# Token slots by float16 products, and graph rows broadcast to 128 partitions

## The chip, the core and the metric

The kernel runs on one core of one Trainium2 chip. The core has five engines with instruction streams of their own, which meet only through semaphores: TensorE (PE in the profile; its weight loads are listed apart, as PEld), VectorE (DVE), ScalarE (ACT), GpSimd (POOL) and SyncE (SP), which here issues DMAs only. SyncE, ScalarE and GpSimd can issue DMAs; 16 DMA engines carry them out. On-chip memory has 128 partitions, and a tile has a row in each partition that it uses. [...]

The metric is the device time of one execution, in microseconds. A profile is a further execution, taken with the hardware profiler; its stretch from the first to the last instruction is called the span.

## The reference, cut to what matters

1250 tokens of 768 features pass through a two-layer graph attention network with 20000 edges, a linear attention, and a mixture of eight experts with two experts for each token. The two parts that the change touches are the graph attention and the choice of experts:

```python
def gat_conv(x, src, dst, W, a_src, a_dst, bias, H, C, n):
    h = (x @ W).reshape(n, H, C)
    s_src = (h * a_src).sum(-1)
    s_dst = (h * a_dst).sum(-1)
    e = jax.nn.leaky_relu(s_src[src] + s_dst[dst], NEG_SLOPE)
    emax = jax.ops.segment_max(e, dst, num_segments=n)
    ee = jnp.exp(e - emax[dst])
    denom = jax.ops.segment_sum(ee, dst, num_segments=n)
    alpha = ee / denom[dst]
    out = jax.ops.segment_sum(alpha[:, :, None] * h[src], dst, num_segments=n)
...
probs = jax.nn.softmax(x @ router_w, axis=-1)
gates, idx = jax.lax.top_k(probs, TOPK_ROUTED)
gates = gates / jnp.sum(gates, axis=-1, keepdims=True)
...
g = jax.nn.silu(jnp.einsum('bsd,edh->bseh', x, w_gate))
u = jnp.einsum('bsd,edh->bseh', x, w_up)
expert_out = jnp.einsum('bseh,ehd->bsed', g * u, w_down)
routed = jnp.einsum('bse,bsed->bsd', dense_g, expert_out)
shared = jax.nn.silu(x @ ws_gate) * (x @ ws_up) @ ws_down
alpha = jax.nn.sigmoid(x @ sg_w + sg_b)
return alpha * shared + (1.0 - alpha) * routed
```

The first graph layer has 4 heads of 192 features, the second 2 heads of 96.

## The kernel before

**Tiling.** The tokens lie in 10 tiles of 125 (`NT`, `TP`), on 125 partitions. The transposed, normalised input `xnT` has 6 chunks of 128 features.

**Order of the work.** The code is written in a tile framework. It tracks what reads and writes each tile, sets the semaphores, and a planner with a cost model of its own sorts the instructions onto each engine when the program is built; an instruction may pass others that stand ahead of it in the source if its inputs come earlier in that plan. On the chip the order on each engine is fixed. So independent products stand interleaved on TensorE, and where the plan is off, an engine waits. A tile with `bufs=2` has two buffers; a third use waits until the first is free.

**Stages.** (1) Normalisation, first graph projection `G` and the counting of edges into the dense tables `cntT` and `absent` (0 to about 212 us in the profile). (2) Keys and values of the linear attention (L542), beside the maximum of the first graph layer's scores on VectorE (L489), to 394 us. (3) Queries and the projection (L572, L585), to 582 us. (4) First graph attention (L602 to L632), to 733 us. (5) Second graph layer, beside the products of the graph's output layer `update` (L724), to 897 us. (6) Router and shared expert (L845 to L951), to 990 us. (7) Blocks of routed tokens (L1003), to 1535 us. (8) Combination and output.

**Graph rows.** Each layer needs a row of scores in every partition. `rows` (L460) transposes columns of scores into rows and stores them to DRAM (`g_srow_d`, `g_rrow_d`). `Largest.head` (L480) reads one such row of 1250 back into 125 partitions as `ssb`; ten instructions of VectorE (L489, in `tile`) add the mask `absent` to it and take each destination's maximum. `columns` turns these into a second set of rows. `attend` (L591) reads two half rows of 625, for each half of the destinations and each head, into the tile `r`, on 125 partitions. `r` and `ssb` share a tag, and so two buffers. For each tile of sources ScalarE takes two exponentials of `r` (`ea` L602, `eb` L604), VectorE their maximum (L605) and the product with the counts (`u`, L607), and TensorE multiplies by `u` (`pa`, L624, in the first layer; `pn`, L740, in the second). Both broadcasts are issued by GpSimd. In the second layer, `some` and `fill` offer the planner products of `update` between these steps.

**Slots.** Each token goes to two experts. The blocks have 128 places each, and there are `NBLK` = 26 blocks at most. VectorE works out from the router's scores the place of each token's two entries, `slot` (L897): block times 128 plus the place in it. The blocks need the inverse: which token stands at each place. For that, a table `who` in DRAM is filled early with a mark for nobody (L329); then 20 indirect DMAs of GpSimd, one for each token tile and choice, write each token's number (and, in a second word, the number of its output row) to its slot (L902), and a DMA of SyncE that waits for all 20 reads the table back as `ids` (L908). `gather` (L975) uses `ids` for an indirect DMA that fetches a block's token rows from DRAM into `xin`, and `down` uses its second word to write the results. While this goes on TensorE computes the shared expert (L946), nine pairs of `pg` and `pu`, each 128 rows of hidden features by 375 or 500 tokens. The pairs have two buffers in PSUM, which ScalarE (L949) and VectorE (L950, L951) empty. The first block begins with the transposes of `xin` (L1009) behind the last shared product.

```python
put = nc.gpsimd.indirect_dma_start(
    out=who, out_offset=bass.IndirectOffsetOnAxis(ap=slot[:, r, t:t + 1], axis=0),
    in_=number[:, r, t, :], in_offset=None, bounds_check=NSLOT - 1, oob_is_err=False)
```

Of the kernel before, what the change touches and what calls it, by code (L numbers as in the profile page):

```python
# [8 lines left out]
F32 = mybir.dt.float32  # L9
F16 = mybir.dt.float16  # L10
# [3 lines left out]
I32 = mybir.dt.int32  # L14
AF = mybir.ActivationFunctionType
ALU = mybir.AluOpType
# [28 lines left out]

NBLK = -(-((NE - 2) * NPART - 2 * (-N // PART)) // NPART)
NSURE = -(-(2 * N + NE * PART // 2) // P)
NSLOT = NBLK * P


CO = H2 * (C2 + 1) + 2 * H2
# [11 lines left out]
def gps_block(ctx: ExitStack, tc: tile.TileContext, x, src, dst, norm_g, norm_b, W1, a_src1, a_dst1, b1,  # L63
# [7 lines left out]


    xd = dram.tile([N, D], F32, name="xd")
    who = dram.tile([NSLOT, 2], I32, name="who")

    ys = dram.tile([2 * N + P - TP, D], F32, name="ys")
    xd_t = xd.rearrange("(t p) d -> t p d", p=TP)
    who_b = who.rearrange("(b p) o -> b (p o)", p=P)
    who_p = who.rearrange("(b p) o -> p b o", p=P)


    acc = big.tile([TP, NT, D], F32, name="acc")
# [240 lines left out]
    with tc.tile_pool(name="cnt", bufs=1, reuse_waits="tile") as cp, \  # L323
            tc.tile_pool(name="tokps", bufs=2, space=PSUM, reuse_waits="tile") as ps, \
            tc.tile_pool(name="cntps", bufs=3, space=PSUM, reuse_waits="tile") as pcp:

        nobody = cp.tile([NBLK, P, 2], I32, name="nobody")
        nc.gpsimd.iota(nobody, pattern=[[0, P], [2 * N, 2]], base=0, channel_multiplier=0)
        nc.sync.dma_start(who_b, nobody.rearrange("b p o -> b (p o)"))  # L329

        rest = cp.tile([P - TP, D], F32, name="rest")
        nc.gpsimd.memset(rest, 0.0)
        nc.sync.dma_start(ys[2 * N:, :], rest)
# [138 lines left out]
    class Largest:  # L472
# [5 lines left out]
            self.mx = p3.tile([TP, NT, H], F32, name=f"{name}_mx")  # L478

        def head(self, h):  # L480
            self.ssb = pmx.tile([TP, N], F32, name="ssb")
            nc.gpsimd.dma_start(self.ssb, bass.AP(tensor=self.srow.tensor, offset=self.srow.offset + h * N,
                                                ap=[[0, TP], [1, N]]))

        def tile(self, h, dt):


            junk = pmx.tile([TP, N], BF16, name="junk", bufs=1)
            nc.vector.tensor_tensor_reduce(out=junk, in0=self.ssb, in1=absent[:, dt, :], scale=1.0,  # L489
                                           scalar=-3.0e38, op0=ALU.add, op1=ALU.max,  # L490
                                           accum_out=self.mx[:, dt, h:h + 1])

# [98 lines left out]
    def attend(pw, ss, ss02, rrow, H, begin, step, finish, fill=lambda half: None):  # L591
        for half in range(2):
            for h in range(H):
                r = pmx.tile([TP, 2, W], F32, name="r", tag="ssb")
                nc.gpsimd.dma_start(r, bass.AP(tensor=rrow.tensor, offset=rrow.offset + h * N + half * W,
                                             ap=[[0, TP], [H * N, 2], [1, W]]))
                sums = begin()
                for st in range(NT):


                    ea = pw.tile([TP, W], F32, name="ea", bufs=2)
                    nc.scalar.activation(ea, r[:, 0, :], AF.Exp, bias=ss[:, st, h:h + 1])  # L602
                    eb = pw.tile([TP, W], F32, name="eb", bufs=2)
                    nc.scalar.activation(eb, r[:, 1, :], AF.Exp, bias=ss02[:, st, h:h + 1])  # L604
                    nc.vector.tensor_max(ea, ea, eb)  # L605
                    u = pw.tile([TP, W], F32, name="u", bufs=3)
                    nc.vector.scalar_tensor_tensor(u, ea, 1.0, cntT[:, st, half * W:(half + 1) * W],  # L607
                                                   op0=ALU.min, op1=ALU.mult)
                    step(sums, st, h, u)
                    fill(half)  # L610
                finish(sums, half, h)
# [203 lines left out]
    with tc.tile_pool(name="fln", bufs=2, reuse_waits="tile") as pw, tc.tile_pool(name="flnps", bufs=2, space=PSUM, reuse_waits="tile") as ps:  # L815
# [11 lines left out]
        odd = pw.tile([TP, -(-NBLK // 2), 2], F32, name="odd", bufs=1)  # L827
        nc.gpsimd.iota(odd, pattern=[[0, -(-NBLK // 2)], [1, 2]], base=0, channel_multiplier=0,
                       allow_small_or_imprecise_dtypes=True)
        rev = pw.tile([TP, NT, NE], F32, name="rev", bufs=1)  # L830
        nc.gpsimd.iota(rev, pattern=[[0, NT], [-1, NE]], base=NE, channel_multiplier=0,
                       allow_small_or_imprecise_dtypes=True)
        number = pw.tile([TP, 2, NT, 2], I32, name="number", bufs=1)
        for r in range(2):
            nc.gpsimd.iota(number[:, r], pattern=[[TP, NT], [r * N, 2]], base=0, channel_multiplier=1)
        for ts in (range(NH2, NH2 + 3), range(NH2 + 3, NT)):
            for _ in normed(ts, pw, ps):
                pass
# [57 lines left out]
            nc.vector.tensor_reduce(at[:, r, :], pick, axis=AX.X, op=ALU.add)  # L896
        nc.vector.tensor_copy(slot, at)  # L897

        puts = []
        for t in range(NT):  # L900
            for r in range(2):
                put = nc.gpsimd.indirect_dma_start(  # L902
                    out=who, out_offset=bass.IndirectOffsetOnAxis(ap=slot[:, r, t:t + 1], axis=0),
                    in_=number[:, r, t, :], in_offset=None, bounds_check=NSLOT - 1, oob_is_err=False)
                for p in puts:
                    tc.declare_no_dep(put.ins, p.ins, reason="slots differ")
                puts.append(put)
        get = nc.sync.dma_start(ids, who_p)  # L908
        for p in puts:
            tc.add_manual_dep(get.ins, p.ins.name, mybir.DependencyInfo(  # L910
                mybir.DependencyClass.Sync, mybir.DependencyReason.DATA), reason="all slots")

# [240 lines left out]
```

## Time and profile before

| what | us |
|---|---|
| median of 3 runs (lowest, highest) | 1602.89 (1601.76, 1603.23) |
| the profiled execution | 1604.71 |
| its span | 1603.0 |
| VectorE busy | 721.8 |
| ScalarE busy | 367.9 |
| GpSimd busy | 136.6 |
| 20 indirect DMAs of the slots (L902), first start to last start | 945.3 to 973.9 |
| one of them on GpSimd, median | 1.19 |
| one `r` on GpSimd (issue), median | 1.15 |
| one `ssb` on GpSimd (issue), median | 0.52 |

The mean granted clock of TensorE was 0.986 of full speed. The page gives busy times, the time cut into 40 slices, the DMA queues, the chain of work that ended last, the costliest groups of instructions, and the DMA issues with their median time to landing. In a group's line `out<-in` are the names of the tiles, then come the shape and the count, the busy time, the mean of one in ns, and after the second bar the idle time of the engine just before them with what ended most of it. In the table by stretch each engine has its busy time and, in brackets, its instructions; the last three columns are the granted clock, the share of the 16 DMA engines in use, and GB/s. In the chain of waits a line has the start, the length and what the time went to.

### The profile page before, as it was taken

To read this page: it belongs to the slowest core of one execution; us is meant where nothing else is said; L and a number is where in the kernel's file an instruction comes from. 1 tells how busy PE (TensorE), PEld (TensorE's weight loads), DVE (VectorE), ACT (ScalarE), POOL (GpSimd) and SP (SyncE) were. 2 spreads that over 40 slices of the span, in tenths; PEclk is the share of its full clock that TensorE was granted. 3 is DMA by queue.
4 is the path that set the end of the run, shared out by engine and by line. 5 is a ranking of instruction groups with operands and counts; after the bars stand their busy time and mean duration, and the time that the engine had idled before them with its cause. 6 is when DMAs were issued, how large, how long until landed. Compare 5 with 4: busy or idle time off the path is not lost.

```text
span 1603.0 us, 18665 instructions
## 1 busy us (share of the span) xinstructions
PE 1524.3 (95%) x7123; PEld 854.2 (53%) x7123; DVE 721.8 (45%) x1339; ACT 367.9 (23%) x630; POOL 136.6 (9%) x177
## 2 busy tenths in 40 slices
PE   6899889998999989999899999999999999999987
PEld 5566544444454668996455554444444444444443
DVE  7889639511535359986599631111111111111116
ACT  3222211111101048871186310101011110111100
POOL 2211000000000000000000133000100001000000
PEclk9999989999999999999999999999999999999998
DMA  7100041000301111102111338588888888888727
GB/s 201 40 1 1 2 130 41 30 0 21 89 12 49 40 34 36 39 17 77 32 53 57 98 89 244 211 313 307 305 311 326 307 308 309 312 320 312 269 100 269
DMA packets 98586, 229.03 MB, mean 143 GB/s; under 512 B 12746, under 2 KB 35402, under 8 KB 98493
## 3 DMA queue, kind: packets, MB, share of 16 engines
q1 hardware_dynamic: 84547, 191.68, 34.8%
q0 software_dynamic: 11744, 35.43, 6.8%
q10 hardware_dynamic: 2202, 0.64, 0.3%
q8 instruction: 63, 1.03, 0.3%
q14 instruction: 30, 0.25, 0.1%
HBM read 212.18 MB, written 16.48 MB: 143 GB/s over the span
## 4 chain that ended last, share of the span: by engine, by line
issue 32%; PE 30%; DVE 11%; DMA 8%; POOL 4%; ACT 3%; POOLq 0%; SPq 0%; DVEq 0%; ACTq 0%
PE pp L542 6%; PE pu L585 5%; PE pq L572 5%; DVE junk L489 4%; DMA ys<-y,ids 4%; PE pa L624 4%; DVE ea L605 2%; PE pn L740 2%; PE pn L577 2%; ACT eb L604 2%; ACT ea L602 1%; POOL xin L976 1%; DVE u L607 1%; PE pds L1043 1%; POOL ys L1034 1%
## 5 line engine op out<-in xcount | busy, mean ns | idle before, releaser
L1003 PE MATMUL pgb<-wg,xT 128*64 128x384 f32 (+1 forms) x1056 | 178.8, 488 | 0.5 <-ACT xT L1010 0.5
L1003 PE MATMUL pdb<-wd,hT 128*64 128x384 f32 (+1 forms) x1056 | 175.1, 488 | 1.5 <-SPq L1083 1.5
L1003 PE MATMUL pub<-wu,xT 128*64 128x384 f32 (+1 forms) x1056 | 174.0, 486 | 0.0
L542 PE MATMUL pp<-wkv,xnT 128*125 128x512 f32 x360 | 161.9, 599 | 0.1
L624 PE MATMUL pa<-G,u 125*125 125x199 f32 x800 | 140.4, 336 | 11.1 <-DVE h L632 6.0
L624 PEld LDWEIGHTS pa<-G,u 125*125 125x125 f32 x800 | 135.6, 189 | 16.2 <-issue 7.2
L1003 PEld LDWEIGHTS pub<-wu,xT 128*64 128x64 f32 x1056 | 75.7, 137 | 94.6 <-issue 94.6
L1003 PEld LDWEIGHTS pdb<-wd,hT 128*64 128x64 f32 x1056 | 74.6, 137 | 91.7 <-issue 86.9
L1003 PEld LDWEIGHTS pgb<-wg,xT 128*64 128x64 f32 x1056 | 73.7, 137 | 90.7 <-issue 89.8
L542 PEld LDWEIGHTS pp<-wkv,xnT 128*125 128x125 f32 x360 | 66.0, 190 | 73.9 <-issue 73.5
L421 PE MATMUL ph<-wg,xnT 128*125 128x400 f32 x240 | 101.4, 529 | 2.4 <-PEq L435 2.4
L1022 DVE TENSOR_TENSOR h<-h,pgb 128x384 f32<-128x384 f32 x44 | 24.4, 555 | 171.6 <-ACT h L1021 171.6
L1033 DVE COPY y<-pdb 128x768 f32<-128x768 f32 x22 | 21.1, 958 | 178.9 <-PE pdb L1003 178.9
L604 ACT ACTIVATE eb<-r,g_ss 125x625 f32<-125x625 f32 x120 | 95.0, 817 | 23.0 <-DVE ea L605 23.0
L605 DVE TENSOR_TENSOR ea<-ea,eb 125x625 f32<-125x625 f32 x120 | 94.0, 804 | 13.0 <-ACT eb L604 7.6
L607 DVE SCALAR_TENSOR_TENSOR u<-ea,cntT 125x625 f32<-125x625 f32 x120 | 94.1, 805 | 12.5 <-PE pa L624 8.0
L489 DVE CUSTOM_DVE_ANT_0 junk<-ssb,absent 125x1250 bf16<-125x1250 f32 x60 | 87.8, 1463 | 13.7 <-DMA ssb<-g_srow_d 12.4
L1021 ACT ACTIVATE h<-pgb 128x384 f32<-128x384 f32 x44 | 21.6, 490 | 307.6 <-PE pgb L1003 307.6
L572 PE MATMUL pq<-xnT,wq 128*128 128x500 f32 (+1 forms) x216 | 81.4, 521 | 4.2 <-DMA wq<-in_L_mix_w_qkv_dram 4.2
L1027 DVE TENSOR_TENSOR h<-h,pub 128x384 f32<-128x384 f32 x44 | 24.4, 554 | 134.4 <-PE pub L1003 134.4
L724 PE MATMUL pu<-wu,xnT 128*125 128x384 f32 x240 | 82.7, 490 | 1.8 <-DVE acc L729 1.8
L585 PE MATMUL pu<-wp,at 128*125 128x384 f32 x240 | 80.4, 488 | 1.0 <-DVE acc L588 1.0
(254 smaller groups left out, 1696.1 us busy)
## 6 DMA issues: line engine op xcount, KB each, us to landing
wg<-in_L_ffn_w_gate_dram SPq DMA_DIRECT2D x22, 2304.0 KB, 9.6
wu<-in_L_ffn_w_up_dram SPq DMA_DIRECT2D x22, 2304.0 KB, 11.0
wd<-in_L_ffn_w_down_dram SPq DMA_DIRECT2D x22, 2304.0 KB, 10.0
yg<-ys SPq DMA_DIRECT2D x10, 768.0 KB, 8.6
r<-g_rrow_d POOLq DMA_DIRECT2D x12, 610.4 KB, 8.5
wq<-in_L_mix_w_qkv_dram SPq DMA_DIRECT2D x18, 384.0 KB, 3.6
wkv<-in_L_mix_w_qkv_dram SPq DMA_DIRECT2D x6, 768.0 KB, 4.4
acc<-in_x_dram POOLq DMA_DIRECT2D x10, 375.0 KB, 9.7
```

The lines of the kernel that those rows point to most:

```text
L421: nc.tensor.matmul(ph[:, :2 * CG], xnT[:, k, tok], wg[:, k, s * 2 * CG:(s + 1) * 2 * CG], start=(k == 0), stop=(k == KD - 1))
L489: nc.vector.tensor_tensor_reduce(out=junk, in0=self.ssb, in1=absent[:, dt, :], scale=1.0, scalar=-3.0e38, op0=ALU.add, op1=ALU.max, accum_ ...
L542: nc.tensor.matmul(pp, xnT[:, k, tok], wkv[:, k, :, :], start=(k == 0), stop=(k == KD - 1))
L572: nc.tensor.matmul(pq[:, :qw], wq[:, k, :], xnT[:, k, tok], start=(k == 0), stop=(k == KD - 1))
L577: nc.tensor.matmul(pn[j][:, :qw], kvb[:, pr, j, :], qs[:, :qw], start=True, stop=True)
L585: nc.tensor.matmul(pu[:, s, :HALF], at[:, k, i * TP:(i + 1) * TP], wp[:, k, s * HALF:(s + 1) * HALF], start=(k == 0), stop=(k == KD - 1))
L604: nc.scalar.activation(eb, r[:, 1, :], AF.Exp, bias=ss02[:, st, h:h + 1])
L605: nc.vector.tensor_max(ea, ea, eb)
L607: nc.vector.scalar_tensor_tensor(u, ea, 1.0, cntT[:, st, half * W:(half + 1) * W], op0=ALU.min, op1=ALU.mult)
L624: nc.tensor.matmul(pa[i][:, :CO + 1], u[:, i * TP:(i + 1) * TP], G[:, st, h, :CO + 1], start=(st == 0), stop=(st == NT - 1))
L724: nc.tensor.matmul(pu[:, :HALF], xnT[:, k, t * TP:(t + 1) * TP], wus[s][:, k, :], start=(k == 0), stop=(k == KD - 1))
L1003: nc.tensor.matmul(pt[part, :HALF], rows[:, k, part], w[:, k, s * HALF:(s + 1) * HALF], start=(k == 0), stop=(k == KD - 1))
```

## The change

Two things are changed.

The table `who`, its filling, the 20 indirect DMAs and the reading back are gone. `slot` is cut into its low seven bits (the place in the block) and the rest (the block). For each of the two choices VectorE compares the places of all tokens with 0 to 127 (`spot`, 125 x 10 x 128 in float16) and the blocks with 0 to 25 (`numb`, 125 x 10 x 26), and multiplies the latter by the token's number plus one. Ten products of TensorE, one for each token tile, add up `spot` transposed times `numb` in `pids`: at each place of each block stands the number plus one of the token there, or zero. A few small instructions of VectorE make `ids` of it.

The tiles `ssb` and `r` have 128 partitions instead of 125, and so have the DMAs that fill them; the instructions that read them use the first 125. `r` is issued by SyncE instead of GpSimd.

```diff
-        nobody = cp.tile([NBLK, P, 2], I32, name="nobody")
-        nc.gpsimd.iota(nobody, pattern=[[0, P], [2 * N, 2]], base=0, channel_multiplier=0)
-        nc.sync.dma_start(who_b, nobody.rearrange("b p o -> b (p o)"))
...
-            self.ssb = pmx.tile([TP, N], F32, name="ssb")
+            self.ssb = pmx.tile([P, N], F32, name="ssb")
             nc.gpsimd.dma_start(self.ssb, bass.AP(tensor=self.srow.tensor, offset=self.srow.offset + h * N,
-                                                ap=[[0, TP], [1, N]]))
+                                                ap=[[0, P], [1, N]]))
...
-                r = pmx.tile([TP, 2, W], F32, name="r", tag="ssb")
-                nc.gpsimd.dma_start(r, bass.AP(tensor=rrow.tensor, offset=rrow.offset + h * N + half * W,
-                                             ap=[[0, TP], [H * N, 2], [1, W]]))
+                r = pmx.tile([P, 2, W], F32, name="r", tag="ssb")
+                nc.sync.dma_start(r, bass.AP(tensor=rrow.tensor, offset=rrow.offset + h * N + half * W,
+                                             ap=[[0, P], [H * N, 2], [1, W]]))
...
+        count16 = pw.tile([TP, P], F16, name="count16", bufs=1)
+        nc.gpsimd.iota(count16, pattern=[[1, P]], base=0, channel_multiplier=0, allow_small_or_imprecise_dtypes=True)
+        number16 = pw.tile([TP, NT], F16, name="number16", bufs=1)
+        nc.gpsimd.iota(number16, pattern=[[TP, NT]], base=1, channel_multiplier=1,
+                       allow_small_or_imprecise_dtypes=True)
...
-        number = pw.tile([TP, 2, NT, 2], I32, name="number", bufs=1)
-        for r in range(2):
-            nc.gpsimd.iota(number[:, r], pattern=[[TP, NT], [r * N, 2]], base=0, channel_multiplier=1)
...
-        puts = []
-        for t in range(NT):
-            for r in range(2):
-                put = nc.gpsimd.indirect_dma_start(
...
-        get = nc.sync.dma_start(ids, who_p)
...
+        cut = pw.tile([TP, 2, 2, NT], I32, name="cut", bufs=1)
+        nc.vector.tensor_single_scalar(cut[:, 0], slot, P - 1, op=ALU.bitwise_and)
+        nc.vector.tensor_single_scalar(cut[:, 1], slot, P.bit_length() - 1, op=ALU.logical_shift_right)
+        cut16 = pw.tile([TP, 2, 2, NT], F16, name="cut16", bufs=1)
+        nc.vector.tensor_copy(cut16, cut)
+        pids = ps.tile([P, 512], F32, name="pids", tag="m")
+        for r in range(2):
+            spot = pw.tile([TP, NT, P], F16, name="spot", tag="xf", bufs=2)
+            nc.vector.tensor_tensor(spot, cut16[:, 0, r, :, None].to_broadcast([TP, NT, P]),
+                                    count16[:, None, :].to_broadcast([TP, NT, P]), ALU.is_equal)
+            numb = pw.tile([TP, NT, NBLK], F16, name="numb", bufs=1)
+            nc.vector.tensor_tensor(numb, cut16[:, 1, r, :, None].to_broadcast([TP, NT, NBLK]),
+                                    count16[:, None, :NBLK].to_broadcast([TP, NT, NBLK]), ALU.is_equal)
+            nc.vector.tensor_tensor(numb, numb, number16[:, :, None].to_broadcast([TP, NT, NBLK]), ALU.mult)
+            for t in range(NT):
+                nc.tensor.matmul(pids[:, r * NBLK:(r + 1) * NBLK], spot[:, t, :], numb[:, t, :], start=(t == 0),
+                                 stop=(t == NT - 1))
+        own = pw.tile([P, 2, NBLK], F32, name="own", bufs=1)
+        nc.vector.tensor_copy(own, pids[:, :2 * NBLK].rearrange("p (r b) -> p r b", r=2))
+        any_ = pw.tile([P, NBLK], F32, name="any", bufs=1)
+        nc.vector.tensor_add(any_, own[:, 0, :], own[:, 1, :])
+
+        nc.vector.tensor_scalar(ids[:, :, 0], any_, -1.0, 0.0, op0=ALU.add, op1=ALU.max)
+        nc.vector.tensor_scalar(own[:, 0, :], any_, 0.0, 3.0 * N, op0=ALU.is_equal, op1=ALU.mult)
+        nc.vector.tensor_scalar(own[:, 1, :], own[:, 1, :], 0.0, float(N), op0=ALU.is_gt, op1=ALU.mult)
+        nc.vector.tensor_add(any_, any_, own[:, 0, :])
+        nc.vector.scalar_tensor_tensor(ids[:, :, 1], any_, -1.0, own[:, 1, :], op0=ALU.add, op1=ALU.add)
```

## The prediction

> **What bounds the kernel now.** I read the page first.
>
> ```profile
> PE 1524.3 (95%) x7123; PEld 854.2 (53%) x7123; DVE 721.8 (45%) x1339; ACT 367.9 (23%) x630; POOL 136.6 (9%) x177
> ```
>
> TensorE (PE) is busy for 1524.3 of 1603.0 us, so about 79 us of the span can be won by filling its gaps; anything that shortens another engine's work counts only where PE stands still for it. Next I asked for busy time by stretch, cut where the diff touches the program: the broadcast rows of the second graph layer (735 to 897 us) and the router with the shared expert (897 to 990 us).
>
> ```profile
> core 0: us, PE busy (x) PEld busy (x) DVE busy (x) ACT busy (x) POOL busy (x), PEclk, DMA share, GB/s
> 795.00:800.00 5.00, 0.01 (x1) 0.01 (x1) 1.69 (x3) 3.28 (x5) 0.00 (x0) 0.71 0.16 48
> 800.00:804.00 4.00, 4.00 (x8) 2.22 (x9) 3.97 (x6) 3.88 (x6) 0.00 (x0) 0.51 0.00 0
> 804.00:860.00 56.00, 55.94 (x190) 32.51 (x189) 53.42 (x99) 38.01 (x52) 2.30 (x2) 1.00 0.16 44
> 860.00:897.00 37.00, 36.41 (x154) 20.84 (x153) 30.34 (x57) 25.37 (x41) 3.48 (x8) 1.00 0.19 53
> 897.00:990.00 93.00, 92.66 (x305) 50.03 (x304) 35.84 (x125) 17.75 (x32) 30.22 (x33) 1.00 0.52 134
> ```
>
> Two things are to be seen. From 800 to 990 us PE is busy for 189.0 of 190 us, so the scatters, which run on POOL at 945 to 975 us, lie wholly beside PE work. And before 800 there is a hole of 5 us with no PE work, followed by 4 us at a granted clock of 0.51. The chain of waits says what the hole is:
>
> ```profile
> 783.83 2.19 DMA g_rrow_d<-g_rrow
> ...
> 786.71 9.92 DMA r<-g_rrow_d
> 796.72 0.82 ACT ea L602
> ...
> 799.99 2.40 PE pn L740 x4
> ```
>
> PE waits for `pn`, that for `u`, that for `ea`, and that for the first row transfer `r`, 9.92 us from issue to landing. The timeline gives PE's wait at 799.99 as 5.44 us.
>
> **The row transfers (L595 to SyncE, 128 partitions).** Why is `r` slow? I set two broadcasts of the same 610 KB beside each other: `r` and `ssb`, both issued by POOL.
>
> ```profile
> r<-g_rrow_d POOLq DMA_DIRECT2D x12, 610.4 KB, 8.5
> ...
> ssb<-g_srow_d POOLq DMA_DIRECT2D x6, 610.4 KB, 5.9
> ```
>
> These are the issues with their median landing in us. And one microsecond of a lone `r`, then one of `ssb`:
>
> ```profile
> 620.00:621.00 1.00, 1.00 (x8) 1.00 (x7) 0.83 (x3) 0.90 (x2) 0.00 (x0) 1.00 0.30 100
> 744.00:745.00 1.00, 1.00 (x5) 0.60 (x4) 0.00 (x0) 0.00 (x0) 0.00 (x0) 1.00 1.05 315
> ```
>
> `r` keeps a DMA share of 0.30, which is 5 of 16 engines; `ssb` keeps all. [...] The nearest row is `ssb` of this layer, on all 16 engines: 4.88 us to its first use in the chain, moving 220 to 240 GB/s at 746 to 748 us, and I take that. `r` then lands at about 786.3 + 4.9 = 791.2 instead of 796.7. From landing to PE's first `pn` are 799.99 - 796.72 = 3.27 us, so `pn` is ready at 794.5, just as PE runs out of other products at 799.99 - 5.44 = 794.55. The hole closes: **-5.44 us**. Bounds: -0.8 (only the issue gets cheaper) and -5.44 (no more idle is there to take).
>
> The clock comes on top. In 800 to 804 us PE is busy all the time at 0.51, which is 4.00 x 0.49 = **-1.95 us** of work that full clock would save; bounds 0 and -1.95. [...]
>
> Does the gain stay? PE is the full engine from there to 990 us, and VectorE, next with 53.42 of 56, starts earlier by the same 5.5. VectorE had 6.7 us free in 860 to 897. So nothing else is late next until the shared expert, and both move together. SyncE's queue: behind the first two `r` of this layer stand only the later `r` and the shared gate weights (813 us, used at 897). In the first layer the early `r` would stand among the `wq` loads (394 to 556 us), which SyncE issues as their buffers come free, and later ones before `wu1` (733.8), which waits for that layer's end anyway. All later `r` are fetched a head, some 19 us, ahead. I cost these at nothing; if a `wq` load falls behind an `r` it is up to 2 us. POOL loses eight long waits and gains only time.
>
> **The score rows (`ssb`, 128 partitions, still POOL).** It already uses all 16 engines. The one place where it matters is the first layer: PE idles 5.77 us near 226 to 232 because VectorE stands at L489 for `ssb`, with `ks` and `vs` queued behind. Broadcast at 16 engines moved at 225 to 241 GB/s there; rows of weights moved at about 350 just before. Bounds: +0.2 us (2.4% more bytes) and -4.3 (the last 4.5 us of transfer shrink to 2.9, and the 2.7 us that half clock costs after this hole, 231.96 to 237.3, go too). Nearest row is `ssb` itself: 0.
>
> **The scatters (L902, L908) against the products.** Removed: 20 indirect DMAs of 1.19 us with 0.30 between, the load of `ids`, the first fill of `who`. What did their end cost?
>
> ```profile
> 973.91 3.66 DMA who<-number,slot
> 977.78 3.63 DMA ids<-who
> 982.26 7.19 DMA xin<-xd,ids
> ```
>
> ```profile
> 989.56 0.82 PEld L1009 LDWEIGHTS ptr<-ident,xin 128*128 128x128 f32 x6 [0.40 <-issue]
> ```
>
> `xin` lands at 989.45, just as the shared expert ends. The weight load waits 0.40 us, of which 0.23 stands before each of the loads ahead of it too. So this chain of 45 us from `slot` (944.4) is hidden but for **-0.2 us**, and the shared expert is the next limit. Block 0's weights were already asked for at 946 us; block 1's move from 979 to about 948 us, and were not late.
>
> Added on VectorE: two compares of 125x1280 float16. The nearest row and its like on PE:
>
> ```profile
> L384 DVE TENSOR_TENSOR los<-lo,steps 125x1000 f16<-125x1000 f16 x20 | 23.8, 1192 | 0.0
> ```
>
> ```profile
> 90.72 0.76 PE L372 MATMUL ptc<-ident,c 125*125 125x125 f16 x10
> 91.31 1.04 PE L397 MATMUL pc<-wide,los 125*125 125x340 f16 x8
> ```
>
> 1.192 us per 1000 gives 1.5 us each; four of 260 elements at 0.43 (between L880, 160 in 0.33, and L916, 416 in 0.59); about eleven small ones at 0.17. Sum 3.0 + 1.7 + 1.9 = 6.6 us. VectorE does 2 us of other work per 10 us there, so `ids` is ready near 955 and `xin` near 964, 25 us before use: nothing. Two more constants on POOL replace two.
>
> Added on PE, which is full: 20 float16 products. Ten transposes start 0.59 us apart as a group, 0.06 each; a pair of 20-column products between others (71.95 to 72.21) costs 0.13 each. So 1.2 to 2.6 us; the first is nearer in kind (a fresh 125-column weight each), with the entries **+1.5 us**. They also add a wait on PE for `spot` and `numb`. Behind them in order stands the shared expert. The router's other such products (L873, L697) stand among L946 with 0.2 us of PE waits in the whole stage, so I take 0; the far end is in the rivals.
>
> **Sum.** -5.44 - 1.95 - 0.2 + 1.5 = -6.1 us. The profiled span, 1603.0, becomes 1596.9 (its execution took 1604.71, so 1.7 lies around the span). The median of the runs, 1602.89, is 0.1 below the span: 1596.8 us. A difference below 0.2%, 3.2 us, can't be told from no change.
>
> **Rivals.**
> - *Score rows get faster too.* Weight rows at 350 GB/s speak for it, the broadcast rate of `ssb` on 16 engines against. All of -4.3: 1592.5 us.
> - *`r` stays slow.* If many rows read from one place are the limit, and not the engine count, only the issue is saved: -0.8 - 0.2 + 1.5 = +0.5, 1603.4 us. For: two `r` at once reach only 205 GB/s at a share of 0.65. Against: the lone `r` at 0.30, and 4.88 us of `ssb`.
> - *The gain is partly given back*: PE's order is fixed by a planner; if it puts more or fewer products into the former hole, or VectorE at 95% can't follow, half of 7.4 goes: 1600.5 us.
> - *Slower: PE stands at the products.* At about 944 us PE takes them in order right behind `slot`, while VectorE still builds `spot` and `numb`: 5.2 us of that chain plus 1.1 of the shared expert's own, 6.3 us idle; half clock for the next 6.8 costs 3.4; with 1.5 of work 11.2, against 7.6 won: 1606.5 us. It decides from 10.8 us of such cost on. Against it: the 0.2 us that PE waits in this stage now.
>
> **Chances.** Forecast 0.50 (own range 1594.6 to 1599.0), score rows 0.15, slow `r` 0.14, half given back 0.08, slower 0.13. Of the half case some counts as no change: faster 0.70, same 0.16, slower 0.14. The range leaves out most of the slower case and the outer end of the fast one: 1591.0 to 1603.8.
>
> **What would show it.** `r` at a DMA share near 1 and about 5 us to land; no PE wait over 1 us before the first L740 and a granted clock of 1.00 there; PE waits at the new products under 1 us; `xin` landed long before its transposes. Wrong it is if the hole stays, or a new one stands at `pids`.

## The result and the profile after

| | before | after |
|---|---|---|
| median, us | 1603.23 | 1597.08 |
| lowest to highest, 5 runs each | 1601.76 to 1603.64 | 1593.59 to 1597.31 |
| span of the profiled execution | 1603.0 | 1595.1 |

The ratio is 0.9957, with a 95% interval from 0.9943 to 0.9972: faster, by 4.5 to 9 us. The forecast was 1596.8 us.

First the page's busy times, in the form read before:

```profile
PE 1525.0 (96%) x7143; PEld 855.7 (54%) x7143; DVE 724.4 (45%) x1355; ACT 367.6 (23%) x630; POOL 98.1 (6%) x144
```

PE is as busy as it was (1524.3), with 20 more instructions. GpSimd has lost 33 instructions and 38.5 us, and none of that shows in the time (slots only, below). So what was won stands as idle time of PE: 78.7 us of the span before, 70.1 now. The mean granted clock of the two profiled executions is nearly the same, 0.986 before and 0.985 now, so the half clock that is saved in the stages below came back elsewhere in this execution. The issues of the two broadcasts, with KB and median us to landing:

```profile
r<-g_rrow_d SPq DMA_DIRECT2D x12, 625.0 KB, 4.0
ssb<-g_srow_d POOLq DMA_DIRECT2D x6, 625.0 KB, 4.8
```

`r` went from 8.5 to 4.0 us, and `ssb`, which was forecast not to move, from 5.9 to 4.8. The timeline at the start of the second layer (start, length, engine, line; in brackets the idle time before and what ended it; L731 was L740, L586 was L595, L593 was L602, L715 and L720 were L724 and L729):

```profile
783.48 0.91 SPq L586 DMA_DIRECT2D r<-g_rrow_d  x2
789.22 0.82 ACT L593 ACTIVATE ea<-r,h 125x625 f32<-125x625 f32 x1 [8.38 <-DMA r<-g_rrow_d]
792.49 1.29 PE L731 MATMUL pn<-u,h 125*97 125x312 f32 x4 [0.65 <-DVE u L598]
```

From the first issue of `r` to its first use are 5.74 us, and to PE's first L731 another 3.27, exactly as before. PE now waits 0.65 us there instead of 5.44, so this hole gave 4.8 us. Another half microsecond was won some 40 us ahead of it, where PE waits for VectorE's sum `acc`, which stands behind the first `ssb` of this layer; before, then after:

```profile
752.40 8.01 PE L724 MATMUL pu<-wu,xnT 128*125 128x384 f32 x24 [1.61 <-DVE acc L729]
749.69 8.01 PE L715 MATMUL pu<-wu,xnT 128*125 128x384 f32 x24 [1.08 <-DVE acc L720]
```

The second layer by stretch (the columns are those of the earlier table: busy times, then the granted clock, the DMA share and GB/s):

```profile
790.00:794.00 4.00, 3.35 (x12) 1.70 (x10) 3.19 (x5) 4.00 (x7) 0.00 (x0) 1.00 0.01 2
794.00:796.00 2.00, 2.00 (x8) 0.99 (x7) 1.97 (x4) 1.88 (x4) 0.00 (x0) 1.00 0.00 0
796.00:852.00 56.00, 55.65 (x188) 31.97 (x187) 54.61 (x100) 38.96 (x54) 0.00 (x0) 1.00 0.17 45
852.00:889.00 37.00, 36.15 (x154) 20.77 (x153) 29.78 (x56) 24.63 (x39) 3.88 (x9) 1.00 0.20 53
889.00:982.00 93.00, 92.56 (x321) 50.00 (x320) 41.26 (x141) 17.76 (x32) 5.88 (x12) 1.00 0.44 156
616.00:617.00 1.00, 1.00 (x8) 1.00 (x7) 1.00 (x2) 1.00 (x2) 0.00 (x0) 1.00 0.97 285
```

The clock stays at 1.00 where it was 0.51. PE is busy for 55.65 of 56 us and 36.15 of 37; the stage is nearly as full as it was (55.94 and 36.41), and begins 7.5 us earlier. The last row is a lone `r` of the first layer: a DMA share of 0.97 and 285 GB/s, where such a row had 0.30 and 100.

The shared expert with the new products, PE's timeline:

```profile
939.83 0.79 PE L955 MATMUL pu<-xnT,wsu 128*128 128x375 f32 x2
940.49 0.41 PE L909 MATMUL pids<-numb,spot 125*128 125x26 f16 x10
940.75 2.14 PE L955 MATMUL pu<-xnT,wsu 128*128 128x375 f32 x6
942.73 0.40 PE L909 MATMUL pids<-numb,spot 125*128 125x26 f16 x10
942.98 1.51 PE L955 MATMUL pu<-xnT,wsu 128*128 128x375 f32 x4
```

No bracket stands at the products, so PE waits for neither `spot` nor `numb`. From the start of each ten to the next shared product are 0.26 and 0.25 us. GpSimd issues the first gather at 944.67 (982.3 before), 37 us ahead of the transposes that use it (982.1).

### The profile page after: what moved, and what is told of

Read it like the earlier page. It is cut to its first block, busy times and chain, and to the rows that moved or that the text cites. A ratio compares the mean times of both kernels' runs of the same rounds, so it can differ in the third digit from the quotient of the medians.

```text
span 1595.1 us, 18670 instructions
## 1 busy us (share of the span) xinstructions
PE 1525.0 (96%) x7143; PEld 855.7 (54%) x7143; DVE 724.4 (45%) x1355; ACT 367.6 (23%) x630; POOL 98.1 (6%) x144
## 5 line engine op out<-in xcount | busy, mean ns | idle before, releaser
L595 ACT ACTIVATE eb<-r,g_ss 125x625 f32<-125x625 f32 x120 | 95.0, 816 | 20.3 <-DVE ea L596 20.3
L715 PE MATMUL pu<-wu,xnT 128*125 128x384 f32 x240 | 82.1, 487 | 1.3 <-DVE acc L720 1.3
```

What stands on the lines that cost most here:

```text
L595: nc.scalar.activation(eb, r[:TP, 1, :], AF.Exp, bias=ss02[:, st, h:h + 1])
L715: nc.tensor.matmul(pu[:, :HALF], xnT[:, k, t * TP:(t + 1) * TP], wus[s][:, k, :], start=(k == 0), stop=(k == KD - 1))
```

## Where the time went, by stage

The start of the same instructions of PE in two traces says how far one kernel is ahead of the other, and the growth of that lead from one such place to the next is what a stage won. Worked out in this way from the trace of each kernel, in us won over before (minus: lost). The starts were read to 0.1 us, so a figure can be off by 0.1. The experiments of the lower rows follow below:

| kernel | to the first `pkv` (221.3) | keys, values (to 394.1) | queries, first attention (to 733.4) | to the first L740 (800.0) | second attention (to 897.4) | to the first transposes of `xin` (989.8) | rest to the last `pds` (1597.8) |
|---|---|---|---|---|---|---|---|
| the change | 1.1 | 2.6 | -1.5 | 5.3 | 1.0 | -0.8 | 0.5 |
| rows only | 0.8 | 2.4 | -0.8 | 5.8 | 0.9 | 0.0 | 1.6 |
| slots only | 2.2 | 0.1 | -0.2 | 0.9 | -0.4 | -0.8 | 0.8 |
| `r` by GpSimd | 2.8 | 2.7 | -1.2 | 4.7 | 1.1 | -0.8 | 1.9 |
| `r` on 125 by SyncE | 1.0 | 2.5 | -1.2 | 3.3 | 0.6 | -0.8 | 0.0 |
| `ssb` on 125 | 1.4 | -0.2 | -0.5 | 4.9 | 0.9 | -0.8 | -0.4 |
| rows first | 2.3 | 8.6 | -0.7 | 5.3 | 1.0 | -0.8 | 0.6 |
| rows only, rows first | 3.7 | 8.5 | -0.2 | 5.4 | 1.0 | 0.0 | 0.5 |
| the change again | 1.1 | 2.4 | -0.5 | 5.6 | 0.9 | -0.8 | -0.3 |
| rows only again | 0.7 | 2.4 | -1.5 | 6.0 | 1.0 | -0.1 | -0.2 |
| the change, a third time | 0.6 | 2.4 | -2.4 | 5.4 | 0.9 | -0.7 | 0.9 |

Four columns repeat: keys and values, the step to L740, the second attention, and the slots. The first, third and last differ by up to 3 us between kernels that are alike there, and between profiles of one and the same kernel. They are the noise in which the rest has to be read.

## Experiments

**Rows only.** Before, with nothing but the row transfers of the change; the scatters stay.

```diff
-            self.ssb = pmx.tile([TP, N], F32, name="ssb")
+            self.ssb = pmx.tile([P, N], F32, name="ssb")
...
-                                                ap=[[0, TP], [1, N]]))
+                                                ap=[[0, P], [1, N]]))
...
-                nc.gpsimd.dma_start(r, bass.AP(tensor=rrow.tensor, offset=rrow.offset + h * N + half * W,
-                                             ap=[[0, TP], [H * N, 2], [1, W]]))
+                nc.sync.dma_start(r, bass.AP(tensor=rrow.tensor, offset=rrow.offset + h * N + half * W,
+                                             ap=[[0, P], [H * N, 2], [1, W]]))
...
```

> The kernel before, with the row part of the change alone: 128 partitions for both broadcasts and r issued by SyncE; the scatters stay. Theory (the rows carry the gain, the products cost a little): 7 to 8.5 us below the kernel before, that is 0.5 to 1 us below the whole change, TensorE's wait before the first product of the second layer under 1.5 us, and the scatters still hidden behind the shared expert, since they too start earlier. Rival (the freed scatter chain carries a part): at most 4 us below the kernel before, because the first block waits for its tokens.

**Slots only.** The change with the row transfers as they were (125 partitions, GpSimd), so the products alone.

```diff
...
-                r = pmx.tile([P, 2, W], F32, name="r", tag="ssb")
-                nc.sync.dma_start(r, bass.AP(tensor=rrow.tensor, offset=rrow.offset + h * N + half * W,
-                                             ap=[[0, P], [H * N, 2], [1, W]]))
+                r = pmx.tile([TP, 2, W], F32, name="r", tag="ssb")
+                nc.gpsimd.dma_start(r, bass.AP(tensor=rrow.tensor, offset=rrow.offset + h * N + half * W,
+                                             ap=[[0, TP], [H * N, 2], [1, W]]))
...
```

> The kernel before, with the slot part alone: float16 products instead of scatters, rows on 125 partitions issued by GpSimd. Theory: within 1.5 us of the kernel before and not below it by more than 0.5, since the scatters lay wholly beside TensorE's work; the 20 products take under 1.5 us of TensorE. Rival (scatters on the path): 3 us or more below the kernel before.

Rows only took 1592.74 us (1591.04 to 1594.75, 5 runs; ratio 0.993, interval 0.9917 to 0.9943), slots only 1602.8 (1600.86 to 1609.84, 14 runs; 0.9997, 0.9988 to 1.0006), beside 1604.02 for before (23 runs). So the gain is that of the rows, and taking 20 scatters away is worth nothing that the interval shows: they were hidden. Rows only won 11.3 us, more than the 7 to 8.5 expected; the runs at the end of this part come back to that. PE's timeline has the hole in the second and not in the first:

```profile
791.84 1.29 PE L740 MATMUL pn<-u,h 125*97 125x312 f32 x4 [0.49 <-DVE u L607]
```

```profile
797.01 2.40 PE L731 MATMUL pn<-u,h 125*97 125x312 f32 x4 [4.66 <-DVE u L598]
```

The first fence is rows only, the second slots only: 0.49 us of waiting against 4.66. In the table by stage, -0.7 or -0.8 us stands under the slots in each kernel with the products and 0.0 or -0.1 in each with the scatters, so the products cost 0.8 us net.

**Which half of the edit of `r`: the issuing engine or the partitions?** Two kernels, each the whole change with one half of that edit undone.

```diff
-                nc.sync.dma_start(r, bass.AP(tensor=rrow.tensor, offset=rrow.offset + h * N + half * W,
+                nc.gpsimd.dma_start(r, bass.AP(tensor=rrow.tensor, offset=rrow.offset + h * N + half * W,
```

> The whole change, but r (on 128 partitions) issued by GpSimd as before. Theory (the number of partitions sets the number of DMA engines): r keeps a DMA share near 1 and lands in about 5 us; TensorE's wait before the first product of the second layer is 0.5 to 2.5 us and the time within 2 us of the whole change. Rival (SyncE's issue carries it): the 5.4 us wait comes back, 6 us above the whole change.

```diff
-                nc.sync.dma_start(r, bass.AP(tensor=rrow.tensor, offset=rrow.offset + h * N + half * W,
-                                             ap=[[0, P], [H * N, 2], [1, W]]))
+                nc.sync.dma_start(r[:TP], bass.AP(tensor=rrow.tensor, offset=rrow.offset + h * N + half * W,
+                                             ap=[[0, TP], [H * N, 2], [1, W]]))
```

> The whole change, but r on 125 partitions, issued by SyncE. Theory: r runs on 5 engines at a share of 0.30 and lands in 7 to 8 us; 3 to 5 us of TensorE's wait come back, with half clock behind it: 4 to 7 us above the whole change. Rival (SyncE's issue carries it): no more than 1 us above it.

They took 1596.55 us (1593.72 to 1602.37, 7 runs; ratio 0.996, interval 0.9946 to 0.9973) and 1598.82 (1594.08 to 1601.18, 9 runs; 0.9965, 0.9954 to 0.9976). The intervals overlap, so the two traces have to tell them apart. A lone `r` of the first layer in each, `r` by GpSimd on 128 first, then SyncE on 125 (columns as in the stretches above):

```profile
615.00:616.00 1.00, 1.00 (x7) 1.00 (x7) 0.83 (x3) 1.00 (x3) 0.00 (x0) 1.00 1.09 380
```

```profile
616.00:617.00 1.00, 1.00 (x7) 1.00 (x7) 1.00 (x3) 1.00 (x2) 0.00 (x0) 1.00 0.32 125
```

The number of partitions sets the rate of a lone `r`, whoever issues: on 128 a share of 1.09 and 380 GB/s here (0.97 and 285 by SyncE, above), on 125 of 0.32 and 125 GB/s (0.30 and 100 by GpSimd). These are shares, not counts of engines, and they hold for `r`: `ssb` on 125 had a share of 0.95 to 1.09 before (225 to 229 us). At the start of the second layer, from the timelines of five kernels:

| issued by, partitions | first issue to first use, us | PE waits before the first L740, us |
|---|---|---|
| GpSimd, 125 (before; slots only) | 10.0; 9.2 | 5.44; 4.66 |
| SyncE, 125 | 8.0 | 2.89 |
| GpSimd, 128 | 6.4 | 1.71 |
| SyncE, 128 (the change; rows only) | 5.7; 5.6 | 0.65; 0.49 |

Against the 5.44 us of before, the partitions alone take 69% of the wait and SyncE alone 47%; together they leave next to nothing. The partitions shorten the way to first use by 2.3 us (SyncE) and by 2.8 to 3.6 (GpSimd), the issuer by 0.7 (128) and 1.2 to 2.0 (125). So the expectation for SyncE on 125 overrated what comes back: 2.2 us of waiting (2.89 less 0.65) instead of 3 to 5, and 1.7 us of time instead of 4 to 7 (against the change in the comparison of the result). Whether the clock falls is the other difference. PE's wait with GpSimd on 128, then with SyncE on 125, and the clock after the latter:

```profile
790.99 1.29 PE L731 MATMUL pn<-u,h 125*97 125x312 f32 x4 [1.71 <-DVE u L598]
794.37 1.29 PE L731 MATMUL pn<-u,h 125*97 125x312 f32 x4 [2.89 <-DVE u L598]
```

```profile
794.00:795.00 1.00, 0.63 (x3) 0.43 (x4) 1.00 (x3) 1.00 (x3) 0.00 (x0) 1.00 0.32 125
795.00:796.00 1.00, 1.00 (x4) 0.61 (x3) 1.00 (x3) 1.00 (x2) 0.00 (x0) 0.77 0.14 55
796.00:797.00 1.00, 1.00 (x3) 0.50 (x2) 0.97 (x3) 0.91 (x3) 0.00 (x0) 0.50 0.00 0
...
798.00:799.00 1.00, 1.00 (x3) 0.57 (x3) 0.90 (x2) 1.00 (x2) 0.00 (x0) 0.52 0.00 0
799.00:800.00 1.00, 1.00 (x5) 0.57 (x4) 1.00 (x2) 0.90 (x2) 0.00 (x0) 1.00 0.02 8
```

The column before the last two is the granted clock: 1.00, 0.77, 0.50, 0.52, 1.00. The 2.89 us without PE work were followed by 3.4 us at half clock, which began 1.2 us after PE was at work again. After the 1.71 us of `r` by GpSimd the rows from 789 to 797 us all have 1.00.

**`ssb` on 125 partitions.** The whole change with only this undone. It tests the term that the forecast set to nothing.

```diff
-            nc.gpsimd.dma_start(self.ssb, bass.AP(tensor=self.srow.tensor, offset=self.srow.offset + h * N,
-                                                ap=[[0, P], [1, N]]))
+            nc.gpsimd.dma_start(self.ssb[:TP], bass.AP(tensor=self.srow.tensor, offset=self.srow.offset + h * N,
+                                                ap=[[0, TP], [1, N]]))
```

> The whole change, but the score rows ssb come on 125 partitions again, as before. Theory (the traces: with 128 partitions the last stretch of the rows moved at about 410 GB/s instead of 230): TensorE's wait for vs in the first layer is 5.5 to 6 us again instead of 4.3, the K and V stage takes 2.5 us longer, the time is 1 to 3 us above the whole change. Rival (the shorter wait there was luck of the run or came from elsewhere): the wait stays at 4.3 us.

1599.23 us (1595.93 to 1600.9, 8 runs; ratio 0.9972, interval 0.9961 to 0.9982; before in this comparison 1603.44). The change itself, in the same comparison (below), had 0.996 (0.9946 to 0.9974). The two overlap; the traces don't. The first two `ssb` of the first layer, in the change and then with 125:

```profile
223.00:224.00 1.00, 1.00 (x3) 0.37 (x2) 0.00 (x0) 0.21 (x1) 0.00 (x0) 1.00 1.12 411
224.00:225.00 1.00, 1.00 (x3) 0.19 (x1) 0.00 (x0) 0.00 (x0) 0.00 (x0) 1.00 1.00 410
225.00:226.00 1.00, 0.09 (x1) 0.00 (x0) 0.44 (x1) 0.00 (x0) 0.00 (x0) 1.00 1.02 415
226.00:227.00 1.00, 0.00 (x0) 0.00 (x0) 1.00 (x2) 0.00 (x0) 0.00 (x0) 1.00 0.32 125
```

```profile
223.00:224.00 1.00, 1.00 (x4) 0.52 (x3) 0.00 (x0) 0.00 (x0) 0.00 (x0) 1.00 1.11 250
224.00:225.00 1.00, 0.85 (x2) 0.01 (x1) 0.00 (x0) 0.00 (x0) 0.00 (x0) 1.00 1.03 240
...
227.00:228.00 1.00, 0.00 (x0) 0.00 (x0) 1.00 (x1) 0.00 (x0) 0.00 (x0) 1.00 0.95 220
```

Both use all 16 engines (shares of 0.95 to 1.12), but 128 partitions move at 410 to 415 GB/s and 125 at 220 to 250. PE's wait for `vs`, behind which this shows, in the same order (third: before):

```profile
229.35 1.20 PE L539 MATMUL pkv<-vs,ks 125*128 125x129 f32 x4 [4.26 <-DVE vs L537]
```

```profile
230.68 1.20 PE L539 MATMUL pkv<-vs,ks 125*128 125x129 f32 x4 [5.83 <-DVE vs L537]
```

```profile
231.96 1.20 PE L548 MATMUL pkv<-vs,ks 125*128 125x129 f32 x4 [5.77 <-DVE vs L546]
```

4.26 us against 5.83 (5.77 before), and the half clock behind it lasts 3.4 us (229.0 to 232.4) against 6.8. In the table by stage the keys and values win 2.4 to 2.7 us in each kernel that differs from before there by the 128 partitions alone, and between -0.2 and 0.1 in the two without. The half microsecond in the second layer is the same thing: PE's wait for `acc` there is 1.69 us in this run and 1.55 in slots only, and 0.64 to 1.28 in the kernels with `ssb` on 128.

**Rows first.** What is left of that hole is 4.26 us and its half clock. The stretches of one microsecond hint at why `ssb`, issued at 219, comes late: in the change the DMA share is 1.01 to 1.11 from 214 to 223 us, at 347 to 421 GB/s, while weights for later, `wp` and the second `wkv`, are under way. This kernel is the change, and lets these two loads wait for the first `ssb` (`first.got` is its DMA, and `behind` makes a load wait for that).

```diff
...
-        weights(wp, w_proj)
...
-                        nc.sync.dma_start(wkv[:, :, j, :], kv_t[:, :, j + 1, pr * P:(pr + 2) * P])
+                        get = nc.sync.dma_start(wkv[:, :, j, :], kv_t[:, :, j + 1, pr * P:(pr + 2) * P])
+                        if pr == 2:
+                            behind(get)
...
+                    if pr == 0 and t == 0:
+                        early_row = first.got
+                        behind(nc.sync.dma_start(wp, w_proj.rearrange("(k p) f -> p k f", p=P)))
```

> The whole change, and the loads of the projection weights (2.3 MB) and of the second K and V weights (1.5 MB) wait until the first score row has landed. Theory (these loads hold up the row's store and the row, and VectorE stands behind it): the row lands about 5 us earlier, TensorE's wait for vs falls from 4.3 us to under 1.5 and the half clock behind it goes; 4 to 6 us below the whole change. Rival (the row's latency is its own): no more than 1.5 us gained, or a loss where the second K and V weights come late.

**Rows only, rows first.** The same on top of rows only, with the scatters.

> The kernel before with the row part of the change and the later weight loads; the scatters stay. Theory: 4 to 6 us below the run with the row part alone, that is 1586.5 to 1589, and 0.5 to 2 us below the whole change with the later loads. Rival (the products are worth more where the rest is faster, since the scatter chain is then late): TensorE waits over 1 us before the first transposes of the blocks, and the time is at or above that of the whole change with the later loads.

**The change again**, in the same comparison.

> The whole change once more, unaltered, on the same chip as the other three: 1595.5 to 1597.5 us by the runs so far. Theory (the two medians of the whole change and of the row part alone, 4.3 us apart, contain chance in the clock's state, since the stages of the traces account for 0.8 us through the products): its median comes out at most 3 us above 1592.7. Rival (the products cost over 3 us): again 1596 us or more.

Rows first took 1588.4 us (1587.61 to 1590.43, 5 runs; ratio 0.9911, interval 0.9896 to 0.9925), the same with scatters 1588.54 (1586.61 to 1590.07, 5 runs; 0.9914, 0.99 to 0.9928), the change 1596.66 (1594.53 to 1597.74, 5 runs; 0.996, 0.9946 to 0.9974). Both of the former beat both kernels of this case, by 15 us and 8 us, more than the 4 to 6 us below the change that were expected. The one with scatters was expected 0.5 to 2 us below the one with products, and isn't. The change came out where its rival had it, at 1596 us or more, which is why the next pair was run. VectorE's wait for the first row in the change, then with rows first, and PE's timeline there, where the hole was:

```profile
225.56 1.46 DVE L480 CUSTOM_DVE_ANT_0 junk<-ssb,absent 125x1250 bf16<-125x1250 f32 x1 [7.15 <-DMA ssb<-g_srow_d]
219.31 1.46 DVE L480 CUSTOM_DVE_ANT_0 junk<-ssb,absent 125x1250 bf16<-125x1250 f32 x1 [2.08 <-DMA ssb<-g_srow_d]
```

```profile
219.46 4.46 PE L539 MATMUL pp<-wkv,xnT 128*125 128x512 f32 x10
223.76 0.61 PE L545 MATMUL pkv<-vs,ks 125*128 125x129 f32 x4
224.20 6.17 PE L539 MATMUL pp<-wkv,xnT 128*125 128x512 f32 x14
```

VectorE gets its first row at 219.31 instead of 225.56, and PE's products stand without a bracket. The loads had held up both steps of the row: GpSimd now waits 2.0 us for its store to DRAM instead of 4.90, and from the issue of `ssb` (214.88; 218.96 in the change) to its first use are 4.4 us instead of 6.6. The stretch from 219 to 239 us, in which PE was busy for 14.23 us before and 15.74 in the change, at a mean clock of 0.83 and 0.91:

```profile
219.00:239.00 20.00, 20.00 (x60) 9.83 (x59) 19.41 (x31) 2.63 (x8) 0.53 (x1) 1.00 0.70 243
```

The loads that were put back cost nothing that shows: PE's one wait for `wq` at the end of the stage is 3.5 us, as in the change.

**Rows only and the change, side by side.** Rows only had come out at 1592.74, the change at 1597.08 and 1596.66: 4 us apart, though the traces give the products 0.8 us. On the other hand the two kernels with rows first don't differ. So both were run once more, together.

> The broadcast rows alone (scatters kept), once more, beside the whole change on the same chip. Theory A, that the products cost next to nothing and the 4 us between these two in the earlier runs are the half-clock stretches' phase, which changes from execution to execution: both within 2 us of each other, near 1595 to 1597. Theory B, that the slot part costs about 4 us somewhere behind the shared expert: this one near 1592.7, the whole change near 1597, at least 3 us apart.

> The whole change, once more, beside the rows alone on the same chip. Theory A: within 2 us of the rows alone. Theory B: 1596 to 1597.5, at least 3 us above the rows alone.

1596.99 us (1595.18 to 1597.55, 6 runs; ratio 0.9951, interval 0.9936 to 0.9967) and 1597.2 (1595.41 to 1600.91, 6 runs; 0.9955, 0.9938 to 0.9973), beside 1605.39 for before (11 runs). Here they don't differ. This pair ran on another chip than the experiments before it. On that first chip the intervals of rows only (0.9917 to 0.9943) and of the change again (0.9946 to 0.9974) lie apart, in different comparisons, though the two with rows first, also there, agree. Where the 4 us come from stays open. The clock on record doesn't account for them: the runs of rows only had mean granted clocks of 0.988 to 0.990 there, those of the change again 0.989 each. And in the two traces of rows only the table differs where it is noisy, by 0.7 us in the third column and 1.8 in the last. The -0.8 us of the stage is all that a trace lays to the products.

## Why the prediction was right, and where it was right by chance

The total is 0.3 us from the forecast. The steps:

- **The hole before L740, -5.44: right.** 4.8 us were won there. The share of the DMA engines goes from 0.30 to 0.97, and the transfer from 8.5 to 4.0 us. That 128 partitions would bring `r` there was the author's estimate, for which no row of before speaks: the `ssb` that it was modelled on had 125. The change and the two experiments with one half undone show it. 0.65 us of waiting is left, as `r` took 5.74 us from issue to first use where 4.88 were forecast. The other 0.5 of the 5.3 us in the table is the wait for `acc`, which belongs to the score rows. The step's lower bound, "-0.8 (only the issue gets cheaper)", was wrong: with SyncE on 125 partitions the wait fell to 2.89 us, by 2.55 (by 1.8 against slots only). The 0.8 in this bound and in the rival with a slow `r` is one issue of `r` by GpSimd, 1.15 us, less one issue by SyncE, 0.37 us (`wq`, before). That SyncE saves this and no more was an estimate, and no run shows it: on 125 the share is the same with either issuer, 0.30 to 0.34, but SyncE brings the first use forward by 1.2 to 2.0 us.
- **The clock, -1.95: right, but nearly half of it was given back.** The clock is 1.00 throughout. The lead over the kernel before is 7.5 us at the first L740 and 9.2 at the ninth (805.41 less 796.17), so 1.7 us came from the clock. By the end of the second attention the lead is 8.5, and the stage as a whole has won 1.0. From 796 to 889 us PE stands still for 1.2 us (93 less 55.65 and 36.15), where the matching 93 us of before had 0.65 (56 and 37 less 55.94 and 36.41): 0.55 us of the gain goes into waiting while VectorE is busy for 54.61 of 56. For the other 0.2 us no row speaks.
- **A hole that closes only in part.** The forecast's sum has no term for it; the expectation for SyncE on 125 had "half clock behind it", and was right: 3.4 us of half clock followed on 2.89 us without PE work, and none on 1.71. Before, PE's last product ahead of the 5.44 us ended at 794.55, and the half clock began at 797.13, 2.6 us later. It lasted 6.83 us, which is the 6.8 that the slower rival counts on. In which cases half clock followed is counted in the last section.
- **The score rows, 0: wrong, and the one term of the sum that failed.** It read: "Nearest row is `ssb` itself: 0." The row showed that all 16 engines were at work at 225 to 241 GB/s, and I took this for the rate of a broadcast. It is the rate of 125 partitions. 128 move at 410 to 415, and the stage won 2.6 us. Nor was the first layer "the one place where it matters": the wait for `acc` in the second won 0.5. The rival that had this at -4.3 had its transfer term right (1.6 us of transfer foreseen, 1.5 less waiting measured) and its clock term too large: it let 2.7 us of half clock go, but here a hole of 4.26 still halved the clock, for 3.4 instead of 6.8 us. Of work that full clock would save, before lost (237.3 - 231.96) / 2 = 2.7, the change loses (232.4 - 229.35) / 2 = 1.5. So 1.5 + 1.2 = 2.7, beside the 2.6 of the table.
- **The products, +1.5 less 0.2: somewhat large.** 0.8 net; 0.26 and 0.25 us of PE time for each ten where 0.6 was taken. VectorE's part was hidden as forecast, and no wait came up, so the slower rival didn't happen.
- **Not in the sum:** 1.5 us lost from the queries to the first attention's end, and 1.1 and 0.5 won in the first and last part. The loss has a place: PE waits 3.5 us for `wq` in both kernels, and the half clock after it lasted 3.4 us before and 6.8 in the change. Three profiles of the change have -1.5, -0.5 and -2.4 in this part, so it isn't a fixed price of the edit.

Without the last point the terms measured make -5.3 - 1.0 - 2.6 + 0.8 = -8.1 us, 2 us more than the -6.1 of the forecast: the missed 3.1 (2.6 and 0.5), less what hole and clock were overrated by, plus 0.5 for the products, which cost less than forecast. The two profiled executions differ by 7.6 us (1604.71 and 1597.16), the medians of the three comparisons by 6.2, 6.8 and 8.2. So the forecast stands at the small end of what was measured, and that the first median met it to 0.3 us is partly luck. Shown are the side, the place of the main gain, and that the slot part wins nothing.

What stays open: why 125 partitions move at little over half the rate of 128 with all 16 engines at work. The packets of the first two `ssb`, 5000 B each in both, took a median of 362 ns before, on 125, and 193 in the change, on 128; that shows where the time is, not the cause.

## What to carry to other kernels

Give a transfer into all partitions 128 of them even if 125 are used: it costs 2.4% more bytes, and such a transfer on its own moved here at 285 to 415 GB/s instead of 100 to 250 (315 in the first microsecond of one). A full DMA share isn't a full rate (1.00 came with 410 GB/s on 128 partitions and with 225 on 125); compare the GB/s of a transfer with the best in the trace before calling its rate a limit. And look at what the DMA engines carry just before a small transfer that others wait for: holding two weight loads back behind the first row won more here, 8 us, than the whole change (6.8 in the same comparison), while 20 scatters beside a full TensorE were worth nothing.

## What the hardware showed that was not expected

- Half clock came in steps of fixed place. In the traces of before and of the change the stretches at half clock, but for the last microseconds, begin and end on a grid of 3.413 us. In the change they begin, among others, at 194.88, 229.01, 392.85, 584.00 and 1556.80 us, which are 10, 48, 56 and 285 times 3.4133 us apart.
- What a step of that grid does to the next can be counted in these two traces. Where PE was busy for less than 0.4 of a step at full clock, half clock followed, 17 times of 17; where it was busy for more than half of it, in 1 of 882; no step lay between. From half clock the next step was full in 16 of 19 cases with PE busy for 0.8 or more, and in none of 8 below. So PE need not stand still for a whole step (1.02 us of work in the first one below), and a wait has no fixed price. The change and the change again, cut at the grid, around the same wait of 3.47 us before the first attention:

```profile
580.59:584.00 3.41, 1.02 (x6) 1.06 (x7) 2.76 (x4) 3.41 (x6) 0.00 (x0) 1.00 0.96 312
584.00:587.41 3.41, 3.41 (x12) 3.41 (x11) 3.27 (x5) 3.41 (x5) 0.00 (x0) 0.50 0.09 33
```

```profile
577.74:581.15 3.41, 1.58 (x5) 0.56 (x3) 1.19 (x2) 1.79 (x3) 0.00 (x0) 1.00 0.15 18
581.15:584.57 3.42, 1.78 (x11) 1.81 (x12) 3.28 (x5) 3.42 (x6) 0.00 (x0) 1.00 0.88 327
584.57:587.98 3.41, 3.41 (x22) 3.41 (x22) 3.27 (x5) 3.31 (x5) 0.00 (x0) 1.00 0.00 0
```

In the first, one step has PE busy for 1.02 us, and half clock follows; in the second the wait falls on two steps with 1.58 and 1.78 us, and none follows. Beyond its own length, one and the same wait costs 1.7 us (half of the 3.41 at half clock) or nothing. The shorter hole in the keys and values fits this count, with 3.4 us of half clock behind it instead of 6.8: PE was busy for 3.08 us of the first half-clock step in the change, for 1.97 before.
- One issue of `r` by GpSimd took 1.15 us (median) on 125 partitions and 0.71 on 128. By SyncE it is the other way, 0.26 on 125 and 0.36 on 128.
